# A one-column fill between the gathers of token rows in a recommendation model's kernel

## The chip, the core and the metric

The kernel runs on one core of one Trainium2 chip. A core has five engines, each with its own instruction queue that it works through in order: TensorE (PE in the profile; its weight loads are listed apart as PEld), VectorE (DVE), ScalarE (ACT), GpSimd (POOL) and SyncE (SP). They agree with each other through semaphores. Data move between the chip's main memory and the on-chip memories by DMA; a DMA is issued by one engine's queue and carried out by 16 DMA engines that all queues share. Matmul results land in a small accumulation memory, PSUM; everything else on the chip lies in SBUF.

The metric is the time on the device in microseconds (us). The kernel before was run 20 times: median 7146.71 us, lowest 7123.92 us, highest 7168.72 us.

## What is computed

A wide-and-deep ranking model for a batch of 16384. For each example it averages 32 word vectors of 300 numbers, averages three sets of 20 small vectors of 64 numbers, looks up four single small vectors, joins all of it and sends it through three dense layers; a "wide" sum of looked-up scalars is added in front of the sigmoid.

```python
tok = word_emb[token_idx].mean(axis=1)          # (B, 32) indices into (50000, 300)
e1 = emb_mh1[mh1_idx].mean(axis=1)              # 20 indices into 1000 rows of 64
...
o4 = emb_oh4[oh4_idx]
emb = jnp.concatenate([tok, e1, e2, e3, o1, o2, o3, o4], axis=1)   # (B, 748)
wide = (wide_mh1[mh1_idx].sum(axis=(1, 2)) + ...)[:, None]
h = jax.nn.relu(emb @ W1 + b1)                  # 748 -> 1024
h = jax.nn.relu(h @ W2 + b2)                    # -> 512
h = jax.nn.relu(h @ W3 + b3)                    # -> 256
return jax.nn.sigmoid(h @ Wd + bd + wide)
```

All of it is float32.

## The kernel before

The batch is cut into 128 tiles of 128 examples, one example per partition. Two very different ways of looking things up run side by side.

**The word vectors are gathered.** `tokens()` is a generator. For each tile it goes through 16 groups of two tokens (`n_groups`, `TOK_GROUP = 2`). For each of the two tokens GpSimd issues one indirect DMA (L224), which fetches one row of 300 float32 for each of the 128 examples, 153.6 kB, into half of a buffer `tok_rows`. There are six such buffers (`bufs=2 * TOK_LAG`), so at most 12 gathers can be ahead of the additions. When more than `TOK_LAG = 3` groups are under way, `add_up()` puts the additions of the oldest group into VectorE's queue (L211, L213, L215): two additions per group, into a sum `own` that lies in PSUM, the last one of a tile into the feature tile `g`. A gather may start when the additions that read its buffer are done, and an addition may start when its gather has landed. In all there are 128 x 32 = 4096 gathers, and nothing else stands in GpSimd's queue after the first microseconds.

**The small tables are looked up by matmul.** All small tables together are 138 slices of 128 rows. They stay in SBUF as `terms`, each float32 split into three bfloat16. For each example VectorE makes one-hot rows (`one_hots()`, L294: `row` for the place within a slice, `slice` for the number of the slice). `counts()` multiplies them per example on TensorE (L312, tile `pc`) and ScalarE copies the counts out as fp8 (L319, `cnt`). `small_sums()` multiplies the counts with `terms` (L337, tile `pg`), and VectorE adds up the three terms (L343).

**The dense layers** (`mlp()`, L378 to L422) run on blocks of 512 examples, four tiles, in float32 (L388, tile `ph`, ScalarE's relu in L397). They are generators too and are fed into the main loop piece by piece.

**The order** is written out by hand (`manual_schedule`). The main loop goes over tiles and, in each tile, over 11 steps (`STEPS`). One step puts into the queues, in this order: the one-hot rows of the next step, the count matmuls of this one, the due gathers and additions (`toks.to(...)`), some matmuls of the small sums of the tile before, and some matmuls of a dense layer. So in VectorE's queue the one-hot rows of a step stand behind the additions of the step before, and each row tile waits until TensorE is done with the one of two steps before (`bufs=2`). In GpSimd's queue the gathers simply follow each other.

Of the kernel before, what the change touches and what calls it, by code (L numbers as in the profile page):

```python
# [8 lines left out]
F32 = mybir.dt.float32  # L9
# [8 lines left out]
P = 128  # L18
# [28 lines left out]
def kernel(  # L47
# [21 lines left out]
    nc = tc.nc  # L69
# [13 lines left out]
    const = ctx.enter_context(tc.tile_pool(name="const", bufs=1))  # L83
# [108 lines left out]
    def load_weights():  # L192
# [7 lines left out]
        for sb, dram in ((wd_sb, wd), (b1_sb, b1), (b2_sb, b2), (b3_sb, b3), (bd_sb, bd)):  # L200
            nc.sync.dma_start(out=sb, in_=dram)

    n_groups = N_TOK // TOK_GROUP
    under_way = []
    features = {}

    def add_up(t, q, rows):

        a, b = rows[:, 0:TOK_D], rows[:, TOK_D : 2 * TOK_D]
        if q == 0:  # L210
            nc.vector.tensor_add(tok_sum, a, b)  # L211
        else:
            nc.vector.tensor_add(tok_sum, tok_sum, a)  # L213
            to = features[t][:, 0:TOK_D] if q == n_groups - 1 else tok_sum
            nc.vector.tensor_add(to, tok_sum, b)  # L215

    def tokens(t, it):


        for q in range(n_groups):  # L220
            rows = tokp.tile([P, TOK_GROUP * TOK_D], F32, name="tok_rows")
            for r in range(TOK_GROUP):
                j = q * TOK_GROUP + r
                nc.gpsimd.indirect_dma_start(  # L224
                    out=rows[:, r * TOK_D : (r + 1) * TOK_D],
                    out_offset=None,
                    in_=word,
                    in_offset=bass.IndirectOffsetOnAxis(ap=it[:, j : j + 1], axis=0),
                )
            under_way.append((t, q, rows))  # L230
            if len(under_way) > TOK_LAG:
                add_up(*under_way.pop(0))
            yield 1
# [242 lines left out]
    for t in range(tiles + 1):  # L476
# [5 lines left out]
        if t < tiles:  # L482
            if s == 0 and t:
                it, sc = next_it, next_sc
            cnt = cp.tile([P, 2, HALF, n_h], FP8, name="cnt", tag="counts")
            toks = Paced(tokens(t, it[:, s, :].bitcast(U32)))
        else:
            last_tokens()
# [76 lines left out]
```

## Time and profile before

| what | value |
|---|---|
| median of 20 runs | 7146.71 us |
| time of the profiled execution | 7126.98 us |
| its span in the profile | 7125.1 us |
| mean granted TensorE clock | 0.902 |
| busy: PE / DVE / ACT / POOL | 80% / 53% / 35% / 55% of the span |
| gathers (q0) | 629.41 MB, 32.9% of 16 DMA engines' span |
| TensorE's and the other engines' instructions (q8, q14) | 5.29 MB and 1.38 MB |
| first and last gather issued | 3.1 us and 7046.2 us after the start |

The profile is one execution. Busy time of an engine is the sum of its instructions' durations; matmuls overlap and their ends are modelled, so a busy TensorE is not one at its peak. A wait is put down to the engine whose semaphore came last; "remote" or "another core or an unknown queue" is a wait whose releaser the profile could not name (there is one core only here), and "issue" is time in which an engine waited for nothing that the profile shows. Times in the timeline count from the start of the span.

### The profile page before, as it was taken

How to read it: one execution, taken by the hardware profiler on the slowest of the kernel's cores; microseconds unless marked ns; L12 is line 12 of the kernel's file. 1: busy time of each engine (PE TensorE's matmuls, PEld its weight loads, DVE VectorE, ACT ScalarE, POOL GpSimd, SP SyncE). 2: the span in 40 equal slices, each digit the busy share in tenths (PEclk: the TensorE clock that was granted, in tenths of full speed). 3: DMA queues.
4: the chain of work that ended last, by engine and by line, in shares of the span. 5: the costliest groups of instructions: out<-in, count | busy, mean ns of one | idle time of the engine just before them, and what ended most of it. 6: DMA issues, size and time to landing. Idle time of an engine off the chain costs nothing.

```text
span 7125.1 us, 104252 instructions
## 1 busy us (share of the span) xinstructions
PE 5669.9 (80%) x41320; PEld 3494.9 (49%) x41320; DVE 3797.6 (53%) x8014; ACT 2467.9 (35%) x1938; POOL 3892.6 (55%) x4103
## 2 busy tenths in 40 slices
PE   4688778778787888778888878877887788878789
PEld 3444444445444444444444444444444444444447
DVE  6555555555555555555555555555555555555553
ACT  4333333333333333333333333333333333333332
POOL 6555555555555555555555555555555555555552
PEclk7899898999899899988989899898898989999999
DMA  5333333333333333333333333333333333333331
GB/s 153 93 92 92 89 91 91 93 91 94 91 91 94 90 91 92 92 90 89 91 92 93 91 91 93 91 89 89 92 91 92 92 90 90 91 95 90 91 86 46
DMA packets 252890, 652.60 MB, mean 92 GB/s; under 512 B 119009, under 2 KB 119524, under 8 KB 252399
## 3 DMA queue, kind: packets, MB, share of 16 engines
q0 software_dynamic: 196608, 629.41, 32.9%
q1 hardware_dynamic: 55791, 16.53, 1.0%
q8 instruction: 323, 5.29, 0.3%
q14 instruction: 168, 1.38, 0.1%
HBM read 645.59 MB, written 0.07 MB: 91 GB/s over the span
## 4 chain that ended last, share of the span: by engine, by line
PE 33%; another core or an unknown queue 21%; DVE 20%; issue 16%; POOL 6%; DMA 2%; ACT 2%; DVEq 0%; POOLq 0%; SPq 0%; ACTq 0%
PE ph L388 15%; PE pg L337 12%; POOL tok_rows L224 6%; PE pc L312 6%; DVE slice L294 5%; DVE own L213 5%; DVE own L215 4%; DVE row L294 2%; DMA tok_rows<-in_word_emb_dram,it 2%; ACT cnt L319 1%; DVE g L343 1%; PE pt L378 1%; DVE own L211 1%; DVE x L379 1%
## 5 line engine op out<-in xcount | busy, mean ns | idle before, releaser
L224 POOL DMA_INDIRECT tok_rows<-in_word_emb_dram,it x4096 | 3891.7, 950 | 3153.9 <-DVE own L215 1644.1
L319 ACT ACTIVATE cnt<-pc 128x1656 fp8e3<-128x1656 f32 (+1 forms) x1408 | 2123.8, 1508 | 3916.0 <-remote 2138.0
L337 PE MATMUL pg<-terms,cnt 128*128 128x195 bf16 x17664 | 2134.7, 270 | 441.4 <-issue 303.6
L337 PEld LDWEIGHTS <-cnt 128*128 128x128 fp8e3 x17664 | 1765.3, 146 | 677.2 <-issue 537.3
L294 DVE TENSOR_TENSOR row<-own,sc 128x768 bf16<-128x768 bf16 (+1 forms) x1408 | 762.4, 542 | 1995.5 <-remote 1398.5
L388 PE MATMUL ph<-x,w_sb 128*128 128x512 f32 (+5 forms) x3264 | 1547.2, 603 | 31.0 <-issue 29.7
L312 PE MATMUL pc<-slice,row 64*128 64x138 bf16 x16384 | 810.6, 234 | 941.5 <-DVE own L213 549.0
L312 PEld LDWEIGHTS <-row 64*128 64x128 bf16 x16384 | 568.1, 99 | 1957.4 <-issue 1353.6
L388 PE MATMUL ph<-h,w_sb 128*128 128x512 f32 (+2 forms) x2720 | 1337.7, 620 | 25.1 <-issue 23.6
L213 DVE TENSOR_TENSOR own<-own,tok_rows 128x300 f32<-128x300 f32 x1920 | 918.6, 478 | 65.8
L215 DVE TENSOR_TENSOR own<-own,tok_rows 128x300 f32<-128x300 f32 x1792 | 857.2, 478 | 61.9
L343 DVE TENSOR_REDUCE g<-pg 128x130 f32<-128x390 f32 (+1 forms) x512 | 261.3, 510 | 1103.5 <-remote 631.8
L388 PEld LDWEIGHTS ph<-x,w_sb 128*128 128x128 f32 (+1 forms) x3264 | 592.3, 203 | 484.1 <-issue 480.7
L294 DVE TENSOR_TENSOR slice<-own,sc 128x828 bf16<-128x828 bf16 (+1 forms) x1408 | 796.7, 566 | 0.0
L388 PEld LDWEIGHTS ph<-h,w_sb 128*128 128x128 f32 x2720 | 510.2, 210 | 411.5 <-issue 409.2
L397 ACT ACTIVATE h<-ph,b_sb 128x512 f32<-128x512 f32 (+2 forms) x476 | 315.1, 662 | 661.7 <-PE ph L388 359.5
L379 DVE TENSOR_SCALAR x<-pt,scale 128x512 f32<-128x512 f32 (+4 forms) x204 | 138.5, 713 | 45.8 <-PE pt L378 43.3
L378 PE MATMUL pt<-ident,g 128*128 128x128 f32 (+1 forms) x768 | 121.0, 305 | 7.0 <-DVE x L379 6.4
L378 PEld LDWEIGHTS pt<-ident,g 128*128 128x128 f32 (+1 forms) x768 | 102.0, 159 | 11.3 <-DVE x L379 10.0
L211 DVE TENSOR_TENSOR own<-tok_rows 128x300 f32<-128x300 f32 x128 | 61.4, 479 | 4.4
L215 DVE TENSOR_TENSOR g<-own,tok_rows 128x300 f32<-128x300 f32 x128 | 60.2, 471 | 4.4
L413 PE MATMUL po<-h,wd_sb 128*1 128x512 f32 (+2 forms) x136 | 61.0, 566 | 0.3
(34 smaller groups left out, 290.3 us busy)
## 6 DMA issues: line engine op xcount, KB each, us to landing
tok_rows<-in_word_emb_dram,it POOLq DMA_INDIRECT x4096
ix<-in_idx_dram SPq DMA_DIRECT2D x128, 32.0 KB
w_sb<-in_W_dram SPq DMA_DIRECT2D x6, 512.0 KB
raw<-in_mh_dram SPq DMA_DIRECT2D x3, 747.5 KB
it<-in_idx_dram SPq DMA_DIRECT2D x32, 64.0 KB
w_sb<-in_W_dram SPq DMA_DIRECT2D x1, 2048.0 KB
raw<-in_mh_dram SPq DMA_DIRECT2D x1, 617.5 KB
out_dram<-h SPq DMA_DIRECT2D x31, 2.0 KB
```

Source lines behind the costliest of these rows:

```text
L213: nc.vector.tensor_add(tok_sum, tok_sum, a)
L215: nc.vector.tensor_add(to, tok_sum, b)
L224: nc.gpsimd.indirect_dma_start(out=rows[:, r * TOK_D : (r + 1) * TOK_D], out_offset=None, in_=word, in_offset=bass.IndirectOffsetOnAxis(ap ...
L294: nc.vector.tensor_tensor(one[:, 0:rows, :].rearrange("p i (n d) -> p i n d", d=2), iota[:, 0:n].rearrange("p (n d) -> p n d", d=2).unsque ...
L312: nc.tensor.matmul(pc[:, f, k // n, at : at + n_h], hot[0][half, k, :], hot[1][half, k, :], start=True, stop=True,)
L319: nc.scalar.activation(cnt[:, :, b : b + rows, :].rearrange("l f (g k) h -> l f g (k h)", g=2), pc[:, :, :, 0 : n * n_h], AF.Copy, scale=0 ...
L337: nc.tensor.matmul(pg[:, j, :], by_slice[:, :, h], terms[:, h, :], start=(h == h0), stop=(h == h1 - 1))
L343: nc.vector.tensor_reduce(g[:, at : at + n * ROW].rearrange("p (f d) -> p f d", f=n), pg[:, 0:n, :].rearrange("p f (c d) -> p f d c", c=3) ...
L378: nc.tensor.transpose(pt[:kk, s * P : (s + 1) * P], chunk(g, k), ident)
L379: nc.vector.tensor_scalar(x[:kk, k, 0:n], pt[:kk, 0:n], scale[:kk, k : k + 1], None, ALU.mult)
L388: nc.tensor.matmul(ph[:, 0:n], weights[:kk, k, m * P : (m + 1) * P], src[:kk, k, 0:n], start=(k == 0), stop=(k == len(kks) - 1),)
L397: nc.scalar.activation(dst[:, m, 0:n], ph[:, 0:n], AF.Relu, bias=bias[:, m : m + 1])
```

## The change

A tile `pause` of one float32 per partition is made once. After every gather that it issues, GpSimd fills it with zeros. Nothing reads it.

```diff
+    pause = const.tile([P, 1], F32, name="pause")
     n_groups = N_TOK // TOK_GROUP
...
                     in_=word,
                     in_offset=bass.IndirectOffsetOnAxis(ap=it[:, j : j + 1], axis=0),
                 )
+                nc.gpsimd.memset(pause, 0.0)
             under_way.append((t, q, rows))
             if len(under_way) > TOK_LAG:
                 add_up(*under_way.pop(0))
```

In GpSimd's queue a fill of 128 x 1 now follows each of the 4096 gathers. From the second on, each fill waits for GpSimd's own semaphore of the fill before it, since both write the same column. The gathers keep the waits that they had. The queues of the other engines hold the same instructions in the same order as before; lines after L202 stand one lower in the changed kernel, those of the gather two lower (it is L226, the fill L232), those behind the fill three lower.

## Prediction

> **What bounds the kernel now.** I read the page first, then the waits, then the timeline around the longest unexplained waits, then the windows over that stretch.
>
> ```profile
> span 7125.1 us, 104252 instructions
> PE 5669.9 (80%) x41320; PEld 3494.9 (49%) x41320; DVE 3797.6 (53%) x8014; ACT 2467.9 (35%) x1938; POOL 3892.6 (55%) x4103
> L224 POOL DMA_INDIRECT tok_rows<-in_word_emb_dram,it x4096 | 3891.7, 950 | 3153.9 <-DVE own L215 1644.1
> ```
>
> TensorE is the fullest engine, yet a fifth of the span it does nothing. GpSimd has no other work than 4096 gathers of 950 ns. Who waits?
>
> ```profile
> ACT cnt L319 <- remote: 2138.0, 382, 12.1
> POOL tok_rows L224 <- DVE own L215: 1644.1, 761, 5.6
> DVE row L294 <- remote: 1398.5, 288, 8.7
> POOL tok_rows L224 <- issue: 860.7, 2723, 1.6
> DVE g L343 <- remote: 631.8, 141, 11.0
> ```
>
> The three lines marked "remote" (time in all, times, the longest) are consumers of TensorE: by the kernel text each waits for a matmul. They wait up to 12.1 us although the matmuls have, by their records, ended. The timeline shows one such case.
>
> ```profile
> 3411.68 0.54 PE L312 MATMUL pc<-slice,row 64*128 64x138 bf16 x12
> ...
> 3413.16 0.94 POOL L224 DMA_INDIRECT tok_rows<-in_word_emb_dram,it  x1 [0.30 <-issue]
> ...
> 3414.41 0.94 POOL L224 DMA_INDIRECT tok_rows<-in_word_emb_dram,it  x1 [0.30 <-issue]
> ...
> 3418.17 0.95 POOL L224 DMA_INDIRECT tok_rows<-in_word_emb_dram,it  x1 [0.30 <-issue]
> 3421.23 1.55 ACT L319 ACTIVATE cnt<-pc 128x1656 fp8e3<-128x1656 f32 x1 [11.28 <-remote]
> 3421.23 0.56 DVE L294 TENSOR_TENSOR row<-own,sc 128x768 bf16<-128x768 bf16 x1 [7.51 <-remote]
> ```
>
> The count matmuls start at 3411.68 and should be done by 3412.2. ScalarE and VectorE, which need just them, both start at 3421.23, 9 us later. In between GpSimd issues gathers 1.25 us apart (0.95 long, 0.30 between), the last ending at 3419.12. The windows (busy time and count of PE, PEld, DVE, ACT and POOL, then clock, DMA share, GB/s) show TensorE dying away inside the run of gathers, at full clock and with the DMA engines half idle:
>
> ```profile
> 3402.90:3407.90 5.00, 5.00 (x39) 2.69 (x39) 4.78 (x15) 2.24 (x2) 2.85 (x3) 1.00 0.23 61
> 3408.10:3413.10 5.00, 5.00 (x56) 3.54 (x51) 4.86 (x10) 1.55 (x1) 3.80 (x4) 1.00 0.46 123
> 3413.10:3418.10 5.00, 2.61 (x11) 1.16 (x10) 0.59 (x2) 0.00 (x0) 3.79 (x4) 1.00 0.48 126
> 3418.10:3420.10 2.00, 0.00 (x0) 0.00 (x0) 0.00 (x0) 0.00 (x0) 0.95 (x1) 1.00 0.48 115
> ```
>
> To see whether this is the rule I went through the trace's semaphore records: a result of TensorE counts as late where its semaphore comes over 0.6 us after the matmul's modelled end, and overlapping lates are joined. That gives 732 stretches, 2514 us, 35% of the span. Then I sorted runs of gathers spaced 1.25 us by length, taking those after a rest of GpSimd of at least 2 us. A late stretch comes in 31 of 116 runs of two, 17 of 24 of four, 175 of 178 of six, 68 of 68 of eight and 89 of 89 of ten. It starts (median) 3.4 to 5.2 us into the run and ends 1.5, 1.7 and 2.1 us after the last gather of a run of six, eight and ten. More than 3 us after GpSimd stopped none is left. So I read it this way: dense gathers hold back TensorE's results; the kernel then stands until GpSimd itself runs out of free buffers, because VectorE, held up behind TensorE, no longer frees any. TensorE is the bound, slowed by its neighbour.
>
> What that costs: with each matmul weighed by its usual step (0.088 us for L337, 0.045 for L312, 0.43 for L388, 0.109 for L378), 27.4% of the matmul work (1383 of 5039 us) starts in the late stretches. The other 3656 us take the 4611 us outside; at that pace the whole takes 4611 x 5039 / 3656 = 6355 us. All late stretches together are thus worth about 770 us.
>
> **The change, part by part.** The tile adds four bytes per partition, nothing. Instruction fetch: TensorE's 5.29 MB for 82640 instructions is 64 bytes each, so 4096 fills add 0.26 MB to the 1.38 MB of the other engines' queue, nothing beside 629 MB. The fill's wait is for the fill before it, at least one gather (1.25 us) ago, against a duration of 0.1 us: it is met when it is reached. Behind the fill stand the next gather and all later ones; after them wait the additions on VectorE, three groups on. SP's queue is not touched.
>
> **The slot.** What a fill between gathers takes is not in the trace; the nearest rows are those before the first gather:
>
> ```profile
> 0.25 0.10 POOL L550 MEMSET const-float32-0.0<- 128x1 f32 x1 [0.25 <-issue]
> 0.28 0.10 POOL L550 MEMSET const-float32-1.0<- 128x1 f32 x1
> ...
> 1.19 0.28 POOL masks.py:199 TENSOR_SCALAR_AFFINE_SELECT ident<-ident 128x128 f32<-128x128 f32 x1
> ```
>
> Fills of this very size take 0.10 us and follow each other by 0.03. Lower bound: the fill hides in the 0.30 between gathers, 0. Upper bound: one more gap of 0.30 and the costliest small row, 0.28, together 0.58. Between them lies 0.03 to 0.40 (gap plus fill); I take 0.15, the fill and a little dispatch, nearest to the fill's own row. The slot goes from 1.25 to 1.40 us, 4096 x 0.15 = 614 us of GpSimd time. What hides it is GpSimd's idle time waiting for VectorE to free buffers: 1644.1 + 307.4 + 129.2 + 98.5 and smaller lines, some 2290 us, 0.56 us a gather. If that cover went, GpSimd would end at 4096 x slot + 82 (3 us ahead of the first gather, 79 from the last to the end): 5816 us at 1.40, still under 6355. The additions sit idle only 66 + 62 + 9 us before them, so today's gathers are early.
>
> **The gain.** How much of the 770 us goes with the wider slot is the real unknown. A simple picture marks 79% of the trace's moments rightly as late or not: each gather brings 1.55 to 1.6 us of something that drains at 1 us per us, and TensorE is late while over 2.2 to 2.4 us are waiting. In it a run at 1.25 piles up 0.30 to 0.35 us a gather, at 1.40 only 0.15 to 0.20: about half. I take half of 770, 385 us. Bounds: nothing (lateness hangs on the number of gathers under way, which stays 12), and all of it. Of 14 late moments in which the next gather came 1.35 to 2.2 us after the last, 13 ended by 1.6 us after that gather, which speaks for the gap; of 12 with 2.2 to 2.6 us only 5 did, which speaks against a simple rule.
>
> Given back: a denser TensorE may be granted less clock (the clock records show 0.5 for 1403 us of the span); if 5% denser work cost 5% more of that, 70 us. Gathers that now come too late: between 0 and as much again as today's idle before additions, 137 us; I take 45, a third. Sum: 7127 - 385 + 70 + 45 = 6857 us against the profiled execution, which lies 20 us under the median of 7146.71; so 6877, say 6880.
>
> The Trainium skill speaks against this reading. "SBUF — State Buffer", section "Who interferes with whom", says that DMA never contends with a compute engine and that PE and ACT wait on no one. By that rule the gathers can't be the cause, the gain is nil, and the sum would be 7127 us. The row of 3421.23 with 89 of 89 runs of ten beside it weighs more with me. "GPSIMD Engine Reference", section 2.1, puts the dispatch of an instruction at tens of cycles; at its 1.2 GHz and, say, 50 cycles that is an estimate of 0.04 us, by which the slot would be 1.39 with the fill's 0.10 us.
>
> **The rivals.**
> (1) Full dispatch: the fill gets its own gap of 0.30, slot 1.65. For it: every gather has that gap, whatever follows. Against: the first fills step by 0.03. Then no run is dense any more, over the 1.55 to 1.6 of the picture, and GpSimd nearly sets the end: 4096 x 1.65 + 82 = 6840, with 20 to the median 6860. Faster too, by another route.
> (2) GpSimd becomes the bound and the kernel slower: place, its queue; price, 0.30 + 0.28 = 0.58, slot 1.83; 4096 x 1.83 + 82 = 7578, with 20 to the median 7598. It decides from a slot of (7127 - 82) / 4096 = 1.72 us, an extra of 0.47. For it: an instruction of another kind between two DMAs may cost a change-over that no row shows. Against: it needs nearly the upper bound.
> (3) No effect: the fill fits into the 0.30, the spacing stays 1.25, and the late stretches stay: 7147.
>
> **How the numbers follow.** Forecast 57%, rival 1 15%, rival 2 18%, rival 3 10%. The likeliest gives 6880; its own range, from a fifth of the 770 us less 50 given back to nine tenths with 50 given back, is 7147 - 104 = 7043 down to 7147 - 643 = 6504. Rival 1 lies within. Upward I reach past rival 3 to 7200, which leaves out most of rival 2 (15%) and a few per cent below 6500. What a measurement here can tell from no change is about 0.2%, 14 us. Faster: 57 + 15 + 2 of rival 3 = 74%; within 0.2%: 7 of rival 3; slower: 18 + 1 = 19%.
>
> **What would show it.** Right: gathers in a run 1.35 to 1.5 us apart; the "remote" lines of L319, L294 and L343 (2138.0 + 1398.5 + 631.8 us) down by a third or more; the idle time of the gathers put down to L215 down from 1644.1; the mean DMA rate up from 92 GB/s. Wrong: spacing of 1.25 (rival 3) or above 1.72 (rival 2); or spacing of 1.4 with the "remote" lines unchanged, by which the density is not the cause; or additions that now wait for their gathers by hundreds of us.

## The result and the profile after

The changed kernel takes 7216.86 us (median of 7 runs, 7195.23 to 7225.97); the kernel before, on the same chip, 7144.81 us. The ratio is 1.0096, with a 95% interval of 1.0083 to 1.0109: slower by about 1%, where 3.7% faster was forecast. The profiled execution took 7207.77 us. Its page:

```profile
span 7206.0 us, 108348 instructions
PE 5722.1 (79%) x41320; PEld 3500.8 (49%) x41320; DVE 3798.6 (53%) x8014; ACT 2468.5 (34%) x1938; POOL 4358.1 (60%) x8199
...
q14 instruction: 200, 1.64, 0.1%
...
L226 POOL DMA_INDIRECT tok_rows<-in_word_emb_dram,it x4096 | 3891.3, 950 | 2766.9 <-DVE own L216 1605.8
...
L232 POOL MEMSET pause<- 128x1 f32 x4096 | 476.9, 116 | 2.5
```

All 4096 fills are there, 116 ns each. They were paid out of GpSimd's idle time: the idle before gathers was 3153.9 us, the span is 80.9 us longer, and 3153.9 + 80.9 - 476.9 = 2757.9, close to the 2766.9 now. VectorE and ScalarE are busy as before. TensorE's 41320 matmuls take 52 us more (5669.9 before), and its idle time grew by 29 us (1455 to 1484, span less busy). The timeline of GpSimd, start and duration of each instruction, shows why the fills cost it nothing:

```profile
3403.32 0.95 POOL L226 DMA_INDIRECT tok_rows<-in_word_emb_dram,it  x1 [0.19 <-issue]
3404.27 0.11 POOL L232 MEMSET pause<- 128x1 f32 x1
3404.57 0.95 POOL L226 DMA_INDIRECT tok_rows<-in_word_emb_dram,it  x1 [0.19 <-issue]
```

The gathers are still 1.25 us apart. Of the 0.30 us that lay between two of them, 0.11 are now the fill and 0.19 are left. Over all runs of gathers the usual spacing is 1.253 us before and after. So the density that the change was forecast to lower is what it was, and the waits (time in all, times, longest) are as they were too:

```profile
ACT cnt L322 <- remote: 2174.9, 377, 13.2
POOL tok_rows L226 <- DVE own L216: 1605.8, 639, 5.0
DVE row L297 <- remote: 1511.4, 289, 11.0
POOL tok_rows L226 <- issue: 636.8, 3009, 1.4
DVE g L346 <- remote: 541.3, 124, 8.2
```

The three "remote" lines add up to 4227.6 us, 4168.3 before. Late stretches, counted as in the prediction, are 738 with 2461 us (34.2% of the span), 732 with 2514 us before. This count has a flaw that matters further down: TensorE signals 2680 results, the trace holds only 2575 of these semaphore records before and 2607 after, and a result whose record is missing counts as late until the next record comes. Where each record is given to one result, in order of time, the late stretches are 36.6% of the span before and 37.0% after: no less either way.

What is different is the granted clock: 0.8914 in the mean over the runs of the changed kernel, 0.900 over those of the kernel before. The clock records know two values, 1.0 and 0.5. In the profiled executions the clock stood at 0.5 for 1546 us, before for 1403. An estimate from the means: matmul work of 5039 us at full clock times (1/0.8914 - 1/0.900) is 54 us, like the 52 us that TensorE is busier, and most of the 72 us lost.

When is the clock halved? The clock records come in steps of 3.4 us. I took each change of the clock and the share of the 3.4 us just before it in which TensorE was busy. In the changed kernel that share is 0.02 to 0.53 (10th to 90th percentile, median 0.32) ahead of a change to 0.5, and 0.89 to 1.00 ahead of a change back to 1.0; in the kernel before 0.00 to 0.50 (0.32) and 0.87 to 1.00. So a TensorE that stands is slowed, and each pause is paid a second time by the work behind it. The Trainium skill says so too, in "TensorE: Matmul & The Clock Gate", Part 1: the clock is gated to half after an idle window of about 3.4 us. Here windows that were a third busy were enough.

### The profile page after: what moved, and what is told of

It is laid out like the page before. It is cut to its first block, busy times and chain, and to the rows that moved or that the text cites. A ratio compares the mean times of both kernels' runs of the same rounds, so it can differ in the third digit from the quotient of the medians.

```text
span 7206.0 us, 108348 instructions
## 1 busy us (share of the span) xinstructions
PE 5722.1 (79%) x41320; PEld 3500.8 (49%) x41320; DVE 3798.6 (53%) x8014; ACT 2468.5 (34%) x1938; POOL 4358.1 (60%) x8199
## 3 DMA queue, kind: packets, MB, share of 16 engines
q0 software_dynamic: 196608, 629.41, 32.5%
q14 instruction: 200, 1.64, 0.1%
## 4 chain that ended last, share of the span: by engine, by line
PE 43%; another core or an unknown queue 22%; DVE 20%; issue 11%; ACT 2%; DMA 2%; POOL 1%; DVEq 0%; SPq 0%; POOLq 0%; ACTq 0%
PE ph L391 20%; PE pg L340 15%; PE pc L315 7%; DVE slice L297 6%; DVE own L214 5%; DVE own L216 4%; DVE row L297 3%; DMA tok_rows<-in_word_emb_dram,it 2%; ACT cnt L322 1%; DVE x L382 1%; DVE g L346 1%; PE pt L381 1%; DVE own L212 1%; POOL tok_rows L226 0%
## 5 line engine op out<-in xcount | busy, mean ns | idle before, releaser
L226 POOL DMA_INDIRECT tok_rows<-in_word_emb_dram,it x4096 | 3891.3, 950 | 2766.9 <-DVE own L216 1605.8
L391 PE MATMUL ph<-x,w_sb 128*128 128x512 f32 (+5 forms) x3264 | 1589.5, 616 | 38.9 <-issue 36.8
L232 POOL MEMSET pause<- 128x1 f32 x4096 | 476.9, 116 | 2.5
```

The lines of the kernel that those rows point to most:

```text
L226: nc.gpsimd.indirect_dma_start(out=rows[:, r * TOK_D : (r + 1) * TOK_D], out_offset=None, in_=word, in_offset=bass.IndirectOffsetOnAxis(ap ...
L232: nc.gpsimd.memset(pause, 0.0)
L391: nc.tensor.matmul(ph[:, 0:n], weights[:kk, k, m * P : (m + 1) * P], src[:kk, k, 0:n], start=(k == 0), stop=(k == len(kks) - 1),)
```

## The experiments

One thing has to be known to read the numbers. On some chips the kernel before takes 7120 to 7145 us, as in the prediction, on others 5261 us. On the latter the kernel before itself was not profiled, but two kernels of the same time were (`bufs4` and `half_rows`, below): TensorE is 97% busy, there are no "remote" waits, and the gathers follow each other almost without rest. What differs between the chips the runs do not show. I call them chips with and without late results. Every ratio below is against the kernel before on the same chip, with its 95% interval. Diffs are from the changed kernel unless said otherwise.

### Is it the tile, or the number of fills?

`tile_only` keeps the tile and fills it once; `per_group` fills once after each group of two gathers.

```diff
     pause = const.tile([P, 1], F32, name="pause")
+    nc.gpsimd.memset(pause, 0.0)
...
-                nc.gpsimd.memset(pause, 0.0)
```

> The tile `pause` is kept, but filled once at the start and not after the gathers. Theory A (the 4096 fills themselves cost the 1%): ratio to before 0.998 to 1.002, mean clock back at about 0.902. Rival B (the new tile moves later tiles in SBUF by a few bytes, and that costs): ratio 1.006 to 1.013, clock about 0.892.

```diff
-                nc.gpsimd.memset(pause, 0.0)
+            nc.gpsimd.memset(pause, 0.0)
             under_way.append((t, q, rows))
```

> One fill after each pair of gathers, 2048 fills in place of 4096. Theory A with a cost in proportion to the fills: ratio 1.003 to 1.007. Rival B (place of tiles): ratio as in the changed kernel, 1.008 to 1.011. Rival C (the fill only shifts the time of the gathers, in no proportion): anything within 0.995 to 1.012, spacing in a run 1.25 us still.

Measured on a chip with late results: `tile_only` 7139.93 us, 0.9991 [0.9975, 1.0007], clock 0.8997; `per_group` 7146.67 us, 0.9997 [0.9979, 1.0015], clock 0.8977. The place of the tiles is not the cause, and 2048 fills cost nothing that can be measured. On this kind of chip the loss comes only with fills in more than every second gap.

### Does a wider slot do what the prediction said?

Four sizes of the fill, `[P, 192]`, `[P, 320]`, `[P, 512]` and `[P, 900]`, and later 384, change one thing only, the distance from one gather to the next (the slot):

```diff
-    pause = const.tile([P, 1], F32, name="pause")
+    pause = const.tile([P, 512], F32, name="pause")
```

> The fill is 512 columns wide instead of one; by the rows of 0.116 us for 128x1 and 0.206 us for 128x128 it should take about 0.45 us, so that the slot of a gather in a run becomes 0.95 + 0.45 to 0.60 = 1.40 to 1.55 us. The forecast's picture (less dense gathers hold TensorE's results back less): late stretches down from 35% of the span to 15 to 25%, ratio 0.94 to 0.98. Rival (lateness hangs on the number of gathers under way, not on their spacing): late stretches stay at 33 to 37%, ratio 1.00 to 1.03.

> The fill is 900 columns wide, by the same rows about 0.75 us, slot 1.70 to 1.85 us; GpSimd alone then needs 4096 x 1.70 to 1.85 + 82 = 7045 to 7660 us. The forecast's picture: late stretches under 8% of the span, the time set by GpSimd at slot x 4096 + 82. Rival (number under way): late stretches above 20%, the time above that sum by 100 us or more.

Both ran on a chip with late results. `fill512`: 6919.22 us, 0.9685 [0.9662, 0.9709], so 3.2% faster. `fill900`: 8200.47 us, 1.1477 [1.1450, 1.1505]. In GpSimd's timeline of `fill512` the fill is longer than the old gap:

```profile
3399.51 0.95 POOL L226 DMA_INDIRECT tok_rows<-in_word_emb_dram,it  x1 [0.17 <-issue]
3400.45 0.55 POOL L232 MEMSET pause<- 128x512 f32 x1
3401.17 0.95 POOL L226 DMA_INDIRECT tok_rows<-in_word_emb_dram,it  x1 [0.17 <-issue]
```

The slot is 1.66 us, wider than the 1.40 to 1.55 that were expected: 0.95 for the gather, 0.55 for the fill, and 0.17 until the next gather. GpSimd is left with 695.7 us of idle time, 0.17 a gather:

```profile
L226 POOL DMA_INDIRECT tok_rows<-in_word_emb_dram,it x4096 | 3915.5, 956 | 695.7 <-issue 619.1
L232 POOL MEMSET pause<- 128x512 f32 x4096 | 2219.1, 542 | 1.9
```

And these are the waits of `fill512`:

```profile
ACT cnt L322 <- PE pc L315: 3125.2, 891, 9.8
DVE own L216 <- DMA tok_rows<-in_word_emb_dram,it: 1842.1, 1672, 3.2
...
ACT cnt L322 <- remote: 6.3, 2, 3.2
```

ScalarE's "remote" wait fell from 2138.0 to 6.3 us. By the prediction's count late stretches fell from 35% to 11% of the span, and even these 11% are hardly lateness: this trace lacks 312 of the 2680 semaphore records, and with each record given to one result 0.3% is left. (`half_rows_b`, on a chip without "remote" waits, has 11% by the first count and none by the second; `fill900` has 8.5%, where under 8% was expected, and none.) But the additions now wait for their gathers (1842.1 us in the second of these lines): GpSimd has become the bound. The prediction's formula for it, 4096 x slot + 82, gives 6881 us against a span of 6900.2; for `fill900`, with a slot of 1.984 us, 8208 against 8198.5. So the mechanism is there, but the slot that frees TensorE is nearly the one at which GpSimd can't keep up.

> The fill is 192 columns wide. From the measured 0.116 us (one column), 0.542 us (512) and the 0.17 us behind it the slot should be 0.95 + 0.275 + 0.17 = 1.395 us, the value that the forecast took for one column. Forecast's picture: late stretches 12 to 25% of the span, GpSimd no bound (4096 x 1.395 + 82 = 5796 us), ratio 0.93 to 0.975. Rival (lateness needs a slot near 1.6 to go): late stretches above 30%, ratio 0.985 to 1.01.

> The fill is 320 columns wide: slot 0.95 + 0.381 + 0.17 = 1.50 us, GpSimd alone 4096 x 1.50 + 82 = 6226 us. Forecast's picture: late stretches 8 to 15% of the span and, GpSimd being no bound, faster than with 512 columns: ratio 0.91 to 0.955. Rival (the gain at 512 columns came only from the gathers following each other without a break): ratio above 0.9685.

> A fill of 384 columns: slot 0.95 + 0.434 + 0.17 = 1.555 us, GpSimd alone 4096 x 1.555 + 82 = 6451 us. Where the kernel before takes about 7120 to 7145 us: by a drain of 1.55 to 1.6 us a gather, late stretches 12 to 25% and ratio 0.945 to 0.975; if they vanish only beyond 1.6, above 25% and 0.97 to 0.985. Where it takes about 5261 us: 1.22 to 1.24, GpSimd sets the end.

These three ran on chips without late results: `fill192` 5855.21 us, 1.1129 [1.1110, 1.1147]; `fill320` 6275.15 us, 1.1926 [1.1906, 1.1946]; `fill384` 6502.46 us, 1.2359 [1.2338, 1.2380]. Here GpSimd sets the end even before (4096 x 1.253 + 82 = 5214 of 5261 us), so every widening is paid in full. The slots were 1.395, 1.50 and 1.555 us, and with 1.66 and 1.984 they fit one rule: the slot is the larger of 1.253 us and 0.95 + fill + 0.17, where a fill takes 0.116 us and 0.83 ns for each further column. One column gives 1.236, under 1.253.

`fill192b` is `fill192` on a chip with late results, the very slot that the prediction had assumed:

> The fill of 192 columns once more, slot 1.395 us. On a chip where the kernel before takes about 5261 us: GpSimd sets the end again, about 5855 us, ratio 1.11. On one where it takes about 7145 us: late stretches 12 to 25% of the span and ratio 0.93 to 0.975 by the forecast's picture; above 30% and 0.985 to 1.01 by the rival that a slot near 1.6 is needed.

Measured 7022.24 us, 0.9863 [0.9845, 0.9882], spacing 1.395 us. Its "remote" waits:

```profile
ACT cnt L322 <- remote: 1808.1, 373, 10.1
DVE row L297 <- remote: 1309.2, 290, 9.5
...
DVE g L346 <- remote: 325.0, 59, 8.8
```

They add up to 3442.3 us, 17% less than before. Late stretches are 724 with 2264 us, 32% of the span, or 36% with each record given to one result. This and the ratio lie where the expectation put the rival, by which a slot near 1.6 is needed. In runs of ten gathers lateness now begins 7.1 us into the run (3.6 before) and lasts 5.1 us (8.4 before). But GpSimd made longer runs (53 of twelve and 11 of fourteen, against 1 and none before), and every one of these has late stretches. The gain is 98 us, where the prediction had 270 net for this slot.

### What does the fill cost where GpSimd is the bound?

`after_again` is the changed kernel itself, on a chip without late results; `part1` fills one partition instead of 128; `mid_group` fills only after the first gather of each group.

> The changed kernel as it is, once more. Chips differ: the kernel before took 7145 us on one and 5261 us on another. Theory S (in the changed kernel GpSimd stands still for 1.17 us more at every 106th gather, some 38 times): where the kernel before takes about 5261 us and GpSimd sets the end, the time grows by 38 x 1.17 = 44 us, ratio 1.006 to 1.010, and the spacing at gathers 113, 219, 325 is about 2.4 us. Where it takes about 7145 us: ratio 1.008 to 1.011. Rival (every gather is a little slower): spacing in a run above 1.26 us throughout.

```diff
-                nc.gpsimd.memset(pause, 0.0)
+                nc.gpsimd.memset(pause[0:1, :], 0.0)
```

> A fill after every gather, on one partition in place of 128. If the 1% comes from what the fill writes: ratio 0.998 to 1.003. If it comes from the instruction as such, or from its semaphore: 1.007 to 1.012.

```diff
-                nc.gpsimd.memset(pause, 0.0)
+                if r == 0:
+                    nc.gpsimd.memset(pause, 0.0)
```

> One column again, but only after the first gather of each pair: 2048 fills, the other half of those in the changed kernel. If the 1% comes from these fills (between two gathers that nothing separates): ratio 1.008 to 1.011. If it comes only with a fill at every gather: 0.998 to 1.003, as after each pair.

Measured: `after_again` 5305.10 us against 5261.62, 1.0082 [1.0065, 1.0099]; `part1` 5304.62 us, 1.0082 [1.0065, 1.0099]; `mid_group` 5262.32 us, 1.0002 [0.9992, 1.0011]. The changed kernel is slower here too, by nearly the same share, though no result of TensorE is late. Its page and GpSimd's timeline show where:

```profile
span 5305.8 us, 108348 instructions
...
PE 5097.0 (96%) x41320; PEld 3165.0 (60%) x41320; DVE 3767.6 (71%) x8014; ACT 2443.9 (46%) x1938; POOL 4354.8 (82%) x8199
```

```profile
154.37 0.95 POOL L226 DMA_INDIRECT tok_rows<-in_word_emb_dram,it  x1 [0.19 <-issue]
155.32 0.11 POOL L232 MEMSET pause<- 128x1 f32 x1
156.81 0.95 POOL L226 DMA_INDIRECT tok_rows<-in_word_emb_dram,it  x1 [1.38 <-issue]
157.75 0.12 POOL L232 MEMSET pause<- 128x1 f32 x1
158.06 0.95 POOL L226 DMA_INDIRECT tok_rows<-in_word_emb_dram,it  x1 [0.19 <-issue]
```

Between the fill at 155.32 and the next gather GpSimd stands for 1.38 us instead of 0.19 and waits for nothing that the profile shows. Such a stop comes ahead of gathers 113, 219, 325 and so on (counted from 0), every 106th, at 37 of 38 such points; between 60 and 5100 us no other gap of GpSimd is longer than 0.5 us. Together they exceed the usual spacing by 44.0 us; the kernel is 43.5 us slower. With a fill in every second gap only, the spacing at these points is 1.251 us and the loss is gone. On these chips, then, the loss is the stops, not the fills' duration: `part1` with 89 ns instead of 118 loses the same. The wider fills have the stops too, and the wider the fill, the shorter they are: 0.93 us beyond the usual spacing in `fill192`, 0.72 in `fill320`, 0.61 in `fill384`, 0.40 in `fill512`, nothing in `fill900`.

`skip_one` leaves out the fill after the last gather of each tile:

```diff
-                nc.gpsimd.memset(pause, 0.0)
+                if j < N_TOK - 1:
+                    nc.gpsimd.memset(pause, 0.0)
```

> As the changed kernel, but the last gather of each tile has no fill behind it: 3968 fills of 4096. Theory S with the reason that GpSimd catches up on something in a gap without a fill: the stops at every 106th gather are gone, ratio 0.998 to 1.003. Rival (the stops come with the number of fills): still a stop about every 109 gathers, ratio 1.006 to 1.011.

Measured 5302.75 us, 1.0077 [1.0060, 1.0094]; 35 of those 37 stops remain. The stops did not go, so a free gap anywhere between two points is not enough. They are missing at points 961 and 2657, and at these the missing fill lay two gathers ahead of the point. A free gap seems to help only near the point.

### Are the stops the loss on a chip with late results as well?

`skip_point` leaves out just the fill two gathers ahead of each point, 39 of 4096:

```diff
-                nc.gpsimd.memset(pause, 0.0)
+                if (t * N_TOK + j) % 106 != 5:
+                    nc.gpsimd.memset(pause, 0.0)
```

> As the changed kernel, but no fill behind gather 111, 217, 323 and so on, every 106th (39 of 4096 left out), each just ahead of a stop. Theory S (the stops are the cost, and a gap without a fill just before the point avoids them): no spacing of about 2.4 us at gathers 113, 219, 325; where the kernel before takes about 5261 us the ratio is 0.999 to 1.002. Where it takes about 7145 us: 0.998 to 1.004 if the stops are the whole of the 1% there too, 1.005 to 1.011 if something else in the fills costs there. Rival (the other 4057 fills cost): 1.006 to 1.011 on either.

It ran on a chip with late results: 7231.35 us against 7120.67, 1.0178 [1.0154, 1.0201]. The changed kernel has the stops on such a chip as well: in its profile further up the median spacing at the 38 points is 2.43 us. In `skip_point` none of them has a stop (median spacing there 1.385 us, 1.355 in the kernel before), and the kernel is still slower. So the stops are not the loss here, though the changed kernel itself was not run on this chip. GpSimd still has some 2000 us of idle time here (2766.9 less 4096 x 0.19) in which 38 stops of about 1.2 us can hide. The clock was 0.8884 against 0.9001; by the estimate above that is 74 of the 111 us. On a chip without late results `skip_point` was not tried.

### Is it the data or the issuing that holds TensorE back?

`half_rows` and `bufs4` start from the kernel before and have no fill. `half_rows` gathers 150 of the 300 columns and adds them twice, so half of each word vector is left out; by the kernel text the unchanged index now counts half rows, so that index i fetches a half of row i/2. There are as many gathers, of half the bytes. `bufs4` gives the gathers four buffers instead of six.

```diff
...
-            rows = tokp.tile([P, TOK_GROUP * TOK_D], F32, name="tok_rows")
+            rows = tokp.tile([P, TOK_GROUP * TOK_D // 2], F32, name="tok_rows")
...
-                    in_=word,
+                    in_=word.rearrange("v (h d) -> (v h) d", h=2),
```

> No fill; each gather fetches 150 numbers of a row in place of 300 (the word vectors are thus not the reference's: half of each row is left out, and each sum takes the fetched half twice), with as many descriptors, as many gathers and additions of the same size. If the kernel before takes about 7145 us: if the amount of data holds TensorE's results back, the late stretches fall below 10% and the ratio is below 0.90; if it is the issuing of gathers, they stay at 30 to 40% and the ratio is 0.98 to 1.02. If the kernel before takes about 5261 us, GpSimd sets the end either way: ratio 0.98 to 1.01.

> Each gather fetches 150 numbers of a row in place of 300 (half of each word vector is left out, each sum takes the fetched half twice); as many gathers, descriptors and additions as before. Where the kernel before takes about 7120 to 7145 us: if the amount of data holds TensorE back, late stretches under 10% of the span and ratio below 0.90; if it is the issuing, 30 to 40% and 0.98 to 1.02. Where it takes about 5261 us: 0.998 to 1.002.

> Each gather fetches 150 numbers of a row in place of 300 (half of each word vector is left out, each sum takes the fetched half twice). Where the kernel before takes about 7120 to 7145 us: if the amount of data holds TensorE back, late stretches under 10% of the span and ratio below 0.90; if it is the issuing, 30 to 40% and 0.98 to 1.02. Where it takes about 5261 us: 0.998 to 1.002.

The first two ran on chips without late results, 5259.74 us, 0.9997 [0.9987, 1.0008], and 5258.81 us, 0.9995 [0.9985, 1.0006]. They tell only that the spacing of 1.25 us does not depend on the bytes. The third ran on a chip with late results: 7119.87 us, 0.9994 [0.9974, 1.0013]. Its page (q0: packets, MB, share of 16 engines) and waits:

```profile
q0 software_dynamic: 196608, 314.83, 17.5%
```

```profile
ACT cnt L324 <- remote: 2327.1, 423, 11.3
DVE row L299 <- remote: 1399.2, 334, 8.5
```

Half the data (629.41 MB before), the same 196608 packets, the same "remote" waits. Late stretches are 2460 us, 34.6% of the span. It is not the amount of data that makes TensorE's results late. The number of gathers or of their packets may be; the two were not told apart.

```diff
-    tokp = ctx.enter_context(tc.tile_pool(name="tok", bufs=2 * TOK_LAG))
+    tokp = ctx.enter_context(tc.tile_pool(name="tok", bufs=TOK_LAG + 1))
```

> No fill; four buffers of gathered rows in place of six, so that at most 8 gathers instead of 12 can be ahead. Where the kernel before takes about 7120 to 7145 us: if the length of a run decides (late stretches start 3.5 to 5 us into a run), runs of ten vanish, late stretches fall from 35% to 15 to 28% and the ratio is 0.94 to 0.985; if only the mean rate of gathers decides, 33 to 37% and 0.99 to 1.02. Where it takes about 5261 us: GpSimd sets the end still, ratio 1.00 to 1.03, the more the less cover there is.

> No fill; four buffers of gathered rows in place of six, at most 8 gathers ahead. Where the kernel before takes about 7120 to 7145 us: if the length of a run decides, late stretches 15 to 28% of the span and ratio 0.94 to 0.985; if only the mean rate decides, 33 to 37% and 0.99 to 1.02. Where it takes about 5261 us: as measured, 1.000 to 1.002.

`bufs4` ran without late results: 5267.23 us, 1.0011 [1.0002, 1.0021]. `bufs4b` ran with them: 7125.33 us, 0.9985 [0.9967, 1.0004]. The idea was shorter runs of gathers; but there were still 102 runs of ten and 23 of twelve, so whether shorter runs help stays untested.

## Why the prediction was wrong

**The slot: the step that failed.** "Fills of this very size take 0.10 us and follow each other by 0.03 [...] I take 0.15, the fill and a little dispatch." Measured: 1.253 us before and after, nothing. The duration was nearly right (0.116 us), and the lower bound, "the fill hides in the 0.30 between gathers", was the answer. I added the fill to a gap that has room for it. `fill192` to `fill900` show the rule: 1.253 us or 0.95 + fill + 0.17, whichever is more. The Trainium skill's dispatch of tens of cycles ("GPSIMD Engine Reference", section 2.1) gave an estimated slot of 1.39 us in the same way, by adding; the measurement decides against both sums, not against the dispatch itself (0.17 us is left after a fill).

**The gain.** With the slot unchanged nothing of the 385 us could come, and the late stretches (2461 against 2514 us) say so. Its mechanism holds in kind: at 1.66 us the "remote" waits are gone on a chip with late results. Its size does not: at 1.395 us the slot brought 98 us, where half of 770 less 115 was taken. The simple picture of something that piles up forgot that GpSimd, which rests less when it is slower, makes longer runs. Whether the lateness ends near 1.55 to 1.6 us stays open, since 1.50 and 1.555 us were run only on chips without it. The 770 us were also too low a price for all late stretches, as far as the two kinds of chip differ in nothing else: without them the kernel takes 5261 us, 1885 less. The pace outside the stretches, from which 6355 us was scaled, was itself slowed: of the 1403 us at half clock about 1000 lie outside them, and TensorE stands there for over 400 us.

**The rule that spoke against.** The rule of "SBUF — State Buffer", section "Who interferes with whom", that DMA never contends with a compute engine, would have given the better number, 7127 us, by chance: it forbids the 3.2% of `fill512`. On chips without late results the traces show nothing against it.

**Given back.** "A denser TensorE may be granted less clock" had the sign wrong. Every wider slot that left TensorE emptier went with a lower clock: on the chips without late results 0.991 at 97% busy (`mid_group`), 0.957 at 90% (`fill192`), 0.944 at 85% (`fill320`), 0.935 at 83% (`fill384`); on the other kind 0.922 at 80% (`fill512`) and 0.858 at 73% (`fill900`). The kernel before has 0.900 at 80% on that kind, so the busy share alone does not fix the clock; the windows ahead of each change of it, above, show what goes before a change. Gathers that come too late were no cost of the change, since the slot did not move.

**Hidden at no cost.** Instruction fetch was right: 0.26 MB more were forecast, and the queue went from 1.38 to 1.64 MB. The fill's own wait was met in time (2.5 us of idle before all fills).

**The rivals.** Rival 3 named what happened to the spacing, with 10%, but its time, 7147 us, is passed by 1%. Rival 2 was not the case here, yet its formula is confirmed where the slot is wide, and on chips without late results GpSimd nearly sets the end already. Rival 1's slot of 1.65 us was, in effect, `fill512`, which reached it by a longer fill and not by a second gap: 6860 by the sum, 6919.22 measured.

**What stays open** is the 1% on the chip of the prediction. Not the tile (`tile_only`), not 2048 fills (`per_group`), not the stops (`skip_point`). It goes with 143 us more at half clock, and the clock is halved where TensorE stands; whether the clock is the cause or a sign of it, and why a fill in every gap brings this, no run shows. Nor is there a width that is faster on both kinds of chip: 512 columns gain 3.2% on one kind of chip, and on the other the formula gives 6881 us against 5261 (384 columns measured 1.2359).

## What to carry to other kernels

Before an instruction between two DMAs is priced, ask what the gap between them already hides: a short one leaves the spacing as it is, and one that outgrows the gap widens it by its excess. (That the spacing stays does not make it free: here one in every gap brought the stops, and a loss of about 1%.) Before a queue is slowed to spare its neighbour, work out the slot at which that queue becomes the bound; here relief (1.395 us gives 1.4%, 1.66 gives 3.2%) and bound (1.72) lie side by side. And a contention seen on one chip should be looked for on a second one before a kernel is tuned around it.

## What the hardware showed that I had not expected

- The same kernel takes 5261 us on some chips and 7120 to 7145 us on others. What the profiles show to differ is TensorE's late results, 35% of the span on the second kind.
- On chips with late results, halving the gathered bytes leaves them at 34.6% of the span, and with a slot of 1.66 us 0.3% is left (36.6% before, counted alike).
- With a one-column fill in every gap GpSimd stops for about 1.2 us ahead of every 106th gather, from gather 113 on, and with one in every second gap it does not. What it does in that time the profile does not name.
- TensorE's granted clock was halved after 3.4 us in which it was about a third busy, and over the kernels it fell from 0.991 to 0.858 as TensorE became emptier.
